# Three moves in one block kernel: attention queries asked for earlier, one stage put in program order, expert weights mixed one convolution earlier

## The chip, the cores and the metric

The kernel runs on one core of one Trainium2 chip. All data is float32. The metric is the device time of one execution in microseconds (us). The engines are named as in the profile: PE is TensorE (matrix products; PEld its weight loads), DVE is VectorE, ACT is ScalarE, POOL is GpSimd, SP is SyncE, which computes nothing and here only issues DMA transfers. Each engine takes its own instructions strictly in the order in which they were written into its stream. PSUM, which PE writes into, has 8 banks; a bank holds 512 float32 numbers in each of 128 partitions.

## What is computed

The input is three images of 256 channels on 48 x 48 pixels (2304 pixels each). Four layers follow, each of the form x = x + layer(norm(x)), where the norm is over 32 groups of channels:

```python
x = x + L0(gn(x))   # cv1 (1x1) + SiLU -> y1, y2; two blocks on y2; cv2 (1x1) on the concatenation + SiLU
x = x + L1(gn(x))   # 3x3 convolution whose kernel is a mix of 8 expert kernels, per image
x = x + L2(gn(x))   # plain 3x3 convolution
x = x + L3(gn(x))   # Mamba: scan over the 2304 pixels

# a block of L0:
cur = cur + attention(norm(cur))          # 4 heads of 32; the batch of 3 is used as q, k, v
cur = cur + f2 @ gelu(f1 @ norm(cur))     # MLP 128 -> 256 -> 128

# the mix of L1, for each image n:
routing = sigmoid(mean(x_n) @ routing_ws)             # 8 numbers
ws_n = sum over e of routing[e] * weight[e]           # 8 kernels of 256 x 256 x 3 x 3
```

A peculiarity of the attention: the leading axis of 3 of the projected tensor is split as if it were (q, k, v), so image 0 gives the queries, image 1 the keys and image 2 the values, and the three thirds of the channels (called g in the kernel) are the three attention problems.

## The kernel before

The layers run one after another. A chunk is 384 pixels of an image (6 chunks), in the attention up to 512.

**Attention (lines 520 to 660).** For each of two blocks there are 15 jobs: three groups g in the order 2, 1, 0, and for each five stretches of queries (four of 512, one of 256; `SCH`). A job goes through 18 groups of 128 keys (9 in the short jobs). In each group PE forms the scores of four heads (line 537), ACT takes the exponential (line 541), DVE adds the exponentials into `part` (line 608), and PE multiplies the exponentials with the values into the bank `acc` (line 550). The program writes "weighted" one group late (`behind`), so that PE has the next scores to do while ACT works. What a job leaves over is finished in the next job, at fixed groups: at group 0 DVE copies `acc` into `o` (line 590), at groups 1 and 3 PE sums the exponentials (`head_sums`, line 562), at group 4 ACT inverts the sums, at 5 DVE normalises, at 7 PE projects (line 506) and DVE adds to `cur` (line 508). The queries of the following job are formed at group 0: one product on PE (line 493) and one DVE instruction that takes it out of PSUM (`q`, line 498). All of `head_sums`, `queries`, `project` and the small norms share one PSUM bank, `ps_m`. In some jobs the statistics of the coming MLP (`mlp_weights`, called `aside`) are computed at groups 9, 11, 13 and so on.

The order of the attention is pinned: `keep_order` ties every instruction of PE, DVE, ACT and POOL to the one before it on the same engine, so each stream follows the program. Where nothing is pinned, a scheduler decides each engine's order.

**Last MLP and cv2 (lines 766 to 826).** For each image in the order 2, 1, 0: six chunks of 384 pixels of the MLP (`hidden`: two products and two Gelu on ACT; `add_back`: two products and one DVE add), then six chunks of cv2 (`concatenated`: eight products over four operands, two Silu on ACT, a POOL addition of the residual `xc`, two DVE statistics). Three of cv2's operands, `yc`, and the residual `xc` are fetched by `parts` two chunks ahead, by DMAs that SP issues. This stage is not pinned. After an image, `routing` computes its norm and its 8 mixing weights. The mixing (`mixed`) is a generator of 50 steps: 48 times, SP loads 384 KB of an expert kernel into one of six buffers (`wst`, line 238) and DVE multiplies and adds it into `u` (lines 262, 264); two last steps transform the kernel (lines 245 to 250). The kernel of image 2 is mixed while image 1 is in this stage, that of image 1 while image 0 is.

**Convolutions (lines 829 to 952).** Layers 1 and 2 use a Winograd transform along the rows. There are six units (layer 1 for images 2, 1, 0, then layer 2), each of two halves of 24 rows. For each half `input_transform` pads on POOL and ACT and makes six transformed inputs with 12 DVE instructions; `output` issues the products (line 888) and adds them into x with DVE. The generator `beside` runs other work next to a unit: next to unit 1 the mixing for image 0, next to unit 2 the loading of layer 2's kernel (`plain`).

**Mamba (from line 955).** It takes the second half of the time, is pinned, and is not touched by the change.

Of the kernel before, what the change touches and what calls it, by code (L numbers as in the profile page):

```python
# [9 lines left out]
F32 = mybir.dt.float32  # L10
# [6 lines left out]
P = 128  # L17
B = 3
HW = 48
# [10 lines left out]
TW = HW // 4  # L30
TAPS = 9
# [49 lines left out]
def net(  # L81
# [120 lines left out]
    def group_norm(b, psum, tag, stats=None):  # L202

        mv, gm, rstd = norm_stats([xs[b][:, ct, :] for ct in range(CT)], gmat, psum, tag, stats)
        sc = small.tile([P, CT], F32, name="gsc", bufs=4)
        nc.vector.tensor_copy(sc, rstd)
        sh = small.tile([P, CT], F32, name="gsh", bufs=4)
        nc.vector.scalar_tensor_tensor(sh, gm, -1.0, rstd, ALU.mult, ALU.mult)
        return mv, sc, sh

# [68 lines left out]

    def routing(b, psum, tag, stats):  # L280

        mv, sc, sh = group_norm(b, psum, tag, stats)
# [3 lines left out]
        nc.vector.tensor_tensor(pooled, pooled, sh, ALU.add)  # L286
        pr = psum.tile([P, 512], F32, tag=tag, name="ps_r")
# [10 lines left out]
    with ExitStack() as l0:  # L298
# [140 lines left out]
        with ExitStack() as p2:  # L439
# [9 lines left out]
            for i in range(NB):  # L449
# [40 lines left out]
                def queries(g, at, n):  # L490
# [6 lines left out]
                    q = work.tile([P, 512], F32, name="q")  # L497
# [14 lines left out]
                def attention(kts):  # L512
# [55 lines left out]
                    q = queries(jobs[0][0], *SCH[0])  # L568
                    old = behind = None
                    asides = {(1, 1): mlp_weights(i, 2), (0, 1): mlp_weights(i, 1)}  # L570
                    for at, job in enumerate(jobs):
# [6 lines left out]
                        for group in range(groups):  # L578
                            p = scores(job, kts[g], q, group)
# [11 lines left out]
                            if group == 0 and at + 1 < len(jobs):  # L591
                                q_next = queries(jobs[at + 1][0], *SCH[jobs[at + 1][1]])
# [10 lines left out]
                            if group == 9 and job == (1, 0):  # L603
                                kts[0] = keys(0)
                            if group >= 9 and group % 2:
                                next(aside, None)
# [10 lines left out]
                        q = q_next  # L617
# [151 lines left out]
        pss = l0.enter_context(tc.tile_pool(name="pss2", bufs=3, space=PSUM))  # L769
        psa = l0.enter_context(tc.tile_pool(name="psa2", bufs=1, space=PSUM))  # L770
        psm = l0.enter_context(tc.tile_pool(name="psm2", bufs=1, space=PSUM))
        wst = late_pool("wst", 6)

        def parts(b, c):

            yc = ypool.tile([P, 3, CH], F32, name="yc")
            nc.sync.dma_start(yc, ycat[b][:, :, c * CH : (c + 1) * CH])
            xc = ypool.tile([P, CT, CH], F32, name="xc")  # L780
            nc.sync.dma_start(
# [4 lines left out]
        def concatenated(b, c, yc, xc, stats):  # L786
# [13 lines left out]
            nc.gpsimd.tensor_tensor(both, both, xc, ALU.add)  # L800
            for m in range(2):
# [3 lines left out]
        mixing = iter(())  # L805
        upools = {}
        for n, b in enumerate(ORDER):
            xs[b] = late_pool(f"x{b}").tile([P, CT, N], F32, name=f"x{b}")
            ahead = []
            held = None  # L810
            for c in range(NCH):
# [4 lines left out]
                if n == 0 and c == 1:  # L816
                    at_once(mlp_weights(i, 0))
                if c >= NCH - 2:
                    ahead.append(parts(b, c - NCH + 2))
                for _ in range(4):  # L820
                    next(mixing, None)
# [4 lines left out]
            for c in range(NCH):  # L826
                if c + 2 < NCH:
                    ahead.append(parts(b, c + 2))
                concatenated(b, c, *ahead.pop(0), stats)
                for _ in range(5):  # L830
                    next(mixing, None)
            curpools[b].close()
            routing(b, psm, "m", stats)
            if n < 2:
                upools[n] = late_pool(f"up{n}")
                mixing = mixed(b, upools[n])


    with ExitStack() as l1:
        vp = l1.enter_context(tc.tile_pool(name="vp", bufs=2))  # L840
        pad = l1.enter_context(tc.tile_pool(name="pad", bufs=1))
# [3 lines left out]

        HR = HW // 2
        HN = HR * TW

        def input_transform(b, h, sc, sh):

            t = pad.tile([P, CT, HR + 2, PW], F32, name="xpad")
            zero = 0 if h == 0 else HR + 1
            nc.gpsimd.memset(t[:, :, zero, :], 0.0)
            for col in (0, PW - 1):
                nc.gpsimd.memset(t[:, :, :, col : col + 1], 0.0)
            lo = 1 if h == 0 else 0
            for ct in range(CT):
                src = xs[b][:, ct, :].rearrange("p (r c) -> p r c", c=HW)
                row = h * HR - 1 + lo
                nc.scalar.activation(  # L860
                    t[:, ct, lo : lo + HR + 1, 1 : PW - 1], src[:, row : row + HR + 1, :],
                    AF.Identity, bias=sh[:, ct : ct + 1], scale=sc[:, ct : ct + 1],
                )
            d = [t[:, :, :, k : k + 4 * TW - 3 : 4] for k in range(6)]
            vt = vp.tile([P, 6, CT, (HR + 2) * TW], F32, name="vt")
            o = [vt[:, i].rearrange("p t (r c) -> p t r c", c=TW) for i in range(6)]
            c = tmp.tile([P, CT, HR + 2, TW], F32, name="wc", bufs=1)
            e = tmp.tile([P, CT, HR + 2, TW], F32, name="we", bufs=1)
            tt, stt = nc.vector.tensor_tensor, nc.vector.scalar_tensor_tensor
            stt(c, d[2], -4.0, d[4], ALU.mult, ALU.add)  # L870
            stt(e, d[1], -4.0, d[3], ALU.mult, ALU.add)
            tt(o[1], c, e, ALU.add)
# [595 lines left out]
```

## Time and profile before

| | us |
|---|---|
| median of 5 runs | 3830.62 (3825.43 to 3839.13) |
| the profiled execution: its time | 3825.59 |
| the profiled execution: its span, first to last instruction | 3823.6 |
| first attention, first scores to last normalisation | about 113 to 737 |
| middle MLP and projections | about 737 to 810 |
| second attention | about 810 to 1430 |
| last MLP and cv2 | about 1430 to 1657 |
| convolutions | 1659 to about 2150 |
| Mamba | about 2150 to 3823 |

Over the whole span PE is busy for 3213.0 us (84%), DVE for 3226.7 (84%), ACT for 2228.3 (58%) and POOL for 1555.0 (41%). These shares are means over stages with different limits, so each stage is read by itself. Reading the lines: an instruction is named by its line, its engine and what it writes and reads (out<-in); "idle before, releaser" is how long its engine had nothing running just before it, and whose completion ended that. PEq, SPq and the like are an engine's sequencer, which issues DMAs and waits.

### The profile page before, as it was taken

The page shows a single profiled execution, that of the slowest core. Times are in us where ns is not written, and L with a number is a line of the kernel's source. Part 1 is how long each engine was busy: PE and PEld are TensorE (multiplying, and loading weights), DVE is VectorE, ACT ScalarE, POOL GpSimd, SP SyncE. Part 2 cuts the span into 40 slices and gives each one's busy share as a digit, 9 for nine tenths or more (in the row PEclk, how much of TensorE's full clock was granted, in tenths as well). Part 3 has the DMA queues.
Part 4 walks back from the last instruction along what each step waited for, and adds up shares of the span by engine and source line. Part 5 has one row for each costly group of instructions (what it writes and reads, how often), then busy time and mean ns, then how long its engine had stood idle before and what let it go on. Part 6 is the DMA issues. An engine that isn't in the chain of part 4 may idle for free. (4 is left out here: it accounts for less than half of the span.)

```text
span 3823.6 us, 45652 instructions
## 1 busy us (share of the span) xinstructions
PE 3213.0 (84%) x17010; PEld 1402.8 (37%) x17010; DVE 3226.7 (84%) x3518; ACT 2228.3 (58%) x3216; POOL 1555.0 (41%) x674
## 2 busy tenths in 40 slices
PE   7999999999999998678799757877778878887874
PEld 4323232432323234356577523333333333333331
DVE  4798889768888985799988349999998999999997
ACT  2787777657877773210000147676677666777663
POOL 0000000000000001100000049999999999999998
PEclk9999999999999999889899878888888888888886
DMA  4000000000000006824100133434343433343441
GB/s 183 3 1 2 1 1 1 22 36 1 2 1 1 1 1 197 302 76 161 38 32 35 59 80 93 111 92 109 100 104 92 108 92 100 101 111 98 105 101 34
DMA packets 149962, 266.50 MB, mean 70 GB/s; under 512 B 23441, under 2 KB 123601, under 8 KB 147170
## 3 DMA queue, kind: packets, MB, share of 16 engines
q1 hardware_dynamic: 149730, 263.49, 24.2%
q8 instruction: 135, 2.21, 0.2%
q14 instruction: 97, 0.79, 0.1%
HBM read 216.31 MB, written 46.89 MB: 69 GB/s over the span
## 5 line engine op out<-in xcount | busy, mean ns | idle before, releaser
L541 ACT ACTIVATE pt<-ps_s 128x1024 f32<-128x1024 f32 x972 | 939.2, 1022 | 257.7 <-PE ps_s L537 239.6
L1336 POOL TENSOR_TENSOR hc<-hs,bc 128x1536 f32<-128x1536 f32 x288 | 991.1, 3442 | 82.1 <-DVE hs L1321 52.8
L608 DVE TENSOR_TENSOR part<-part,pt 128x2048 f32<-128x2048 f32 x396 | 906.8, 2290 | 104.5 <-ACT pt L541 77.1
L1321 DVE TENSOR_TENSOR_SCAN hs<-ps_da,hst,hs 128x384 f32<-128x384 f32 x960 | 909.5, 997 | 24.3 <-ACT ps_da L1265 20.9
L1265 ACT ACTIVATE ps_da<-dtr,amat 128x384 f32<-128x384 f32 x1152 | 657.3, 581 | 359.9 <-DVE hs L1321 343.3
L158 POOL TENSOR_TENSOR rstd<-ve,mhalf 128x2 f32<-128x2 f32 (+1 forms) x26 | 17.7, 682 | 1680.3 <-DVE ve L156 1680.3
L537 PE MATMUL ps_s<-q,kt 32*128 32x512 f32 (+1 forms) x4320 | 613.9, 593 | 1.8 <-DVE q L498 0.9
L1253 POOL TENSOR_TENSOR hs<-dtur,bc 128x768 f32<-128x768 f32 x288 | 523.8, 1819 | 77.1 <-DMA dtr<-dtd 77.1
L550 PE MATMUL acc<-pt,vt 128*32 128x512 f32 (+1 forms) x4320 | 522.2, 562 | 3.3 <-DVE o L590 3.1
L888 PE MATMUL ps_c<-vt,u 128*128 128x288 f32 x1728 | 430.1, 412 | 35.7 <-DVE u L250 31.8
L1066 PE MATMUL ps_g<-xn,wtap 128*128 128x384 f32 x1152 | 393.1, 494 | 36.4 <-ACT u L1073 31.2
L888 PEld LDWEIGHTS ps_c<-vt,u 128*128 128x128 f32 x1728 | 331.8, 193 | 128.7 <-DVE u L250 32.8
L537 PEld LDWEIGHTS ps_s<-q,kt 32*128 32x128 f32 x4320 | 219.6, 183 | 389.0 <-issue 234.9
L1281 PE MATMUL ps_y<-hc,rep 128*32 128x384 f32 x2304 | 294.9, 598 | 37.1 <-POOL hc L1336 35.2
L1252 DVE TENSOR_TENSOR hs<-ps_r,bc 128x768 f32<-128x768 f32 x288 | 268.7, 933 | 60.5 <-PE ps_r L1234 60.5
L1066 PEld LDWEIGHTS ps_g<-xn,wtap 128*128 128x128 f32 x1152 | 213.2, 190 | 220.8 <-ACT u L1073 54.9
L550 PEld LDWEIGHTS acc<-pt,vt 128*32 128x32 f32 x4320 | 97.5, 108 | 354.6 <-issue 339.4
L904 ACT COPY cb<-ps_c 128x288 f32<-128x288 f32 x48 | 19.0, 395 | 334.6 <-PE ps_c L888 324.9
L1321 DVE TENSOR_TENSOR_SCAN hs<-ps_da,hs 128x384 f32<-128x384 f32 x192 | 170.5, 935 | 16.1 <-ACT ps_da L1265 16.1
L1137 PE MATMUL ps_g<-xn,w3sb 128*128 128x384 f32 x288 | 130.9, 596 | 57.5 <-ACT sz L1145 43.2
L1030 PE MATMUL ps_g<-xg,mean 128*128 128x384 f32 x72 | 52.7, 887 | 105.2 <-ACT dt L1128 78.2
L1281 PEld LDWEIGHTS ps_y<-hc,rep 128*32 128x32 f32 x2304 | 51.5, 118 | 241.1 <-POOL hc L1336 112.3
(204 smaller groups left out, 3263.1 us busy)
## 6 DMA issues: line engine op xcount, KB each, us to landing
wconv<-in_we SPq DMA_DIRECT2D x144, 384.0 KB, 4.6
dtr<-dtd SPq DMA_DIRECT2D x288, 192.0 KB, 3.6
bc<-bcd SPq DMA_DIRECT2D x144, 192.0 KB, 5.8
dtur<-dtud SPq DMA_DIRECT2D x288, 96.0 KB, 2.7
dtd<-dt SPq DMA_DIRECT2D x18, 768.0 KB, 3.5
yc<-ycat SPq DMA_DIRECT2D x18, 576.0 KB, 5.3
xb<-in_x SPq DMA_DIRECT2D x6, 1152.0 KB, 11.2
xc<-in_x SPq DMA_DIRECT2D x18, 384.0 KB, 7.1
```

Of the source, the lines that this page charges most:

```text
L537: nc.tensor.matmul(s[:, j, cols], kt[r, mt * P : (mt + 1) * P], q[r, :n], start=True, stop=True,)
L541: nc.scalar.activation(p[:, h0 : h0 + 2, :], s, AF.Exp)
L550: nc.tensor.matmul(acc[h * HD : (h + 1) * HD, :n], vt[:, mt, g * P + h * HD : g * P + (h + 1) * HD], p[:, h, cols], start=mt == 0, stop=mt ...
L608: nc.vector.tensor_tensor(part, first_p if group == 1 else part, p, ALU.add)
L888: nc.tensor.matmul(pc[:, :HN], u[:, i, dy, ct, m * P : (m + 1) * P], vt[:, i, ct, dy * TW : dy * TW + HN], start=ct == 0 and dy == 0, stop ...
L1066: nc.tensor.matmul(bank[:, m % 2, :CH], wtap[:, tap, ct, m * P : (m + 1) * P], k.xn[:, ct, tap : tap + CH], start=tap == 0 and ct == 0, st ...
L1252: nc.vector.tensor_tensor(hs[:, 0:2, :], k.ps[:, :, :CH], bb, ALU.mult)
L1253: nc.gpsimd.tensor_tensor(hs[:, 2:4, :], k.rows[m][1], bb, ALU.mult)
L1265: nc.scalar.activation(da[:, :CH], chunks[at].rows[m][0][:, q, :], AF.Exp, scale=amat[:, col : col + 1])
L1281: nc.tensor.matmul(k.y_ps[32 * q : 32 * q + 32, :CH], fold, hc[:, q, :], start=False, stop=g == 3,)
L1321: nc.vector.tensor_tensor_scan(hs[:, q, :], decays[q][:, :CH], hs[:, q, :], 0.0 if k.c == 0 else state[m, g][:, q : q + 1], ALU.mult, ALU.add,
L1336: nc.gpsimd.tensor_tensor(hc, hs, cb, ALU.mult)
```

## The change

1. The queries of a job are formed at group 10 of the job before it, no longer at group 0. A short job has only 9 groups; so the fourth long job of a third, which precedes it, also forms those of the job after the short one, at group 13. A third buffer holds them. The asides move from groups 9, 11, 13, ... to 11, 13, ..., and `keys(0)` from group 9 to 11.
2. The last MLP and cv2 stage is pinned with `keep_order`. `parts` is issued by ACT instead of SP, three chunks ahead over the images' borders, and first of all for three chunks at the stage's start. The PSUM banks are dealt out anew (two pairs instead of three for the products; three banks instead of one for `acc`). The statistics of a chunk are written behind the next chunk's products. `routing` and `mlp_weights` become generators, of which each chunk runs one step (`aside`).
3. In that stage only the kernel of image 2 is mixed, at 2 steps per chunk of the MLP and 3 per chunk of cv2, from the moment that its routing is known. The kernel of image 1 is mixed beside unit 0 (image 2), and that of image 0 beside unit 1, as before. The first input transform (image 2, first half) is moved into the stage, to the fourth cv2 chunk of image 0.

The diff, cut to its core (`input_transform` itself is moved in the file and unchanged but for the pool of its two scratch tiles):

```diff
+            yield          # in routing, after `pooled`; its norm is a generator too
...
-                    q = work.tile([P, 512], F32, name="q")
+                    q = work.tile([P, 512], F32, name="q", bufs=3)
...
-                    q = queries(jobs[0][0], *SCH[0])
+                    asked = {}
+                    def ask(at):
+                        if at < len(jobs):
+                            g, c = jobs[at]
+                            asked[at] = queries(g, *SCH[c])
+                    ask(0)
...
-                            p = scores(job, kts[g], q, group)
+                            p = scores(job, kts[g], asked[at], group)
...
-                            if group == 0 and at + 1 < len(jobs):
-                                q_next = queries(jobs[at + 1][0], *SCH[jobs[at + 1][1]])
...
-                            if group == 9 and job == (1, 0):
+                            if group == 10:
+                                ask(at + 1)
+                            if group == 13 and c == len(SCH) - 2:
+                                ask(at + 2)
+                            if group == 11 and job == (1, 0):
                                 kts[0] = keys(0)
-                            if group >= 9 and group % 2:
+                            if group >= 11 and group % 2:
                                 next(aside, None)
...
-        pss = l0.enter_context(tc.tile_pool(name="pss2", bufs=3, space=PSUM))
-        psa = l0.enter_context(tc.tile_pool(name="psa2", bufs=1, space=PSUM))
+        pss = l0.enter_context(tc.tile_pool(name="pss2", bufs=2, space=PSUM))
+        psa = l0.enter_context(tc.tile_pool(name="psa2", bufs=3, space=PSUM))
...
-            nc.sync.dma_start(yc, ycat[b][:, :, c * CH : (c + 1) * CH])
+            nc.scalar.dma_start(yc, ycat[b][:, :, c * CH : (c + 1) * CH])
             xc = ypool.tile([P, CT, CH], F32, name="xc")
-            nc.sync.dma_start(
+            nc.scalar.dma_start(
                 xc, x[b, :, c * CH : (c + 1) * CH].rearrange("(t p) n -> p t n", p=P)
             )
...
+        mark = listed[-1]
+        chunks = [(b, c) for b in ORDER for c in range(NCH)]
+        ahead = [parts(*chunks[z]) for z in range(3)]
+        small_steps = [mlp_weights(i, 0)]
+        mixing = mixed(2, upools[0])
+        def aside(n):
+            if small_steps:
+                try:
+                    next(small_steps[0])
+                except StopIteration:
+                    del small_steps[0]
+            if 2 in route:
+                for _ in range(n):
+                    next(mixing, None)
         for n, b in enumerate(ORDER):
             held = None
             for c in range(NCH):
                 f = hidden(b, c)
                 if held is not None:
                     add_back(i, *held)
                 held = b, c, f
-                if n == 0 and c == 1:
-                    at_once(mlp_weights(i, 0))
-                if c >= NCH - 2:
-                    ahead.append(parts(b, c - NCH + 2))
-                for _ in range(4):
-                    next(mixing, None)
+                aside(2)
             add_back(i, *held)
...
             for c in range(NCH):
-                if c + 2 < NCH:
-                    ahead.append(parts(b, c + 2))
-                concatenated(b, c, *ahead.pop(0), stats)
-                for _ in range(5):
-                    next(mixing, None)
-            curpools[b].close()
-            routing(b, psm, "m", stats)
-            if n < 2:
-                upools[n] = late_pool(f"up{n}")
-                mixing = mixed(b, upools[n])
+                concatenated(b, c, *ahead.pop(0))
+                z = n * NCH + c + 3
+                if z < len(chunks):
+                    ahead.append(parts(*chunks[z]))
+                if c:
+                    take_stats(b, c - 1, stats)
+                if b == 0 and c == 3:
+                    vp = late_pool("vp", 2)
+                    pad = late_pool("pad")
+                    first_v = input_transform(2, 0, *norms[2])
+                aside(3)
+            take_stats(b, NCH - 1, stats)
+            if b:
+                curpools[b].close()
+            small_steps.append(routing(b, psm, "m", stats))
+        for _ in mixing:
+            pass
+        keep_order(tc, listed, mark)
+        for steps in small_steps:
+            at_once(steps)
...
-        beside = {1: mixed(ORDER[2], upools[0]), 2: plain(upools[1])}
+        beside = {0: mixed(1, upools[1]), 1: mixed(0, upools[0]), 2: plain(upools[1])}
...
-        vt = transformed(0)
+        vt = first_v
```

## The prediction

> **What bounds the kernel now.** I read the busy shares by slices first, then the waits of each stage, then the order of instructions at the places that the change touches, and last the busy time of DVE over the stretch that the mixing spans. The Mamba stage (from 2150 us) keeps its instructions and their order; nothing is summed there.
>
> The attention: its waits (first attention; us in total, times, longest), then two borders between jobs in order of time (start, us, engine, what, idle before).
>
> ```profile
> PE ps_m L562 <- DVE q L498: 17.3, 10, 2.1
> ...
> 202.77 0.68 DVE L590 COPY o<-acc 128x512 f32<-128x512 f32 x1
> 203.37 0.74 DVE L498 TENSOR_SCALAR q<-ps_m,qkb 128x512 f32<-128x512 f32 x1
> 204.16 1.06 PE L562 MATMUL ps_m<-pt,ones 128*32 128x512 f32 x8 [1.64 <-DVE q L498]
> 204.53 2.29 DVE L608 TENSOR_TENSOR part<-pt 128x2048 f32<-128x2048 f32 x1 [0.42 <-ACT pt L541]
> ...
> 710.81 0.68 DVE L590 COPY o<-acc 128x512 f32<-128x512 f32 x1
> ...
> 711.54 1.09 PE L550 MATMUL acc<-pt,vt 128*32 128x256 f32 x16 [1.57 <-DVE o L590]
> ```
>
> PE hardly ever waits inside a job; at each border it waits some 1.7 us, because `head_sums` needs the bank that DVE has not yet emptied of the queries. The last border (711 us) has no queries, and there PE waits 1.57 us all the same: for `o`, which DVE copies only when its additions are done. So DVE's lag is behind the wait, and the queries only stand in front of it.
>
> The cv2 stage and the first convolutions: waits of the stage, then waits of the convolutions, then busy time from the first mixing instruction to unit 2's first product.
>
> ```profile
> PE ps_s L790 <- DMA yc<-ycat: 30.1, 6, 14.3
> ...
> SPq L238 <- DVE u L264: 65.3, 71, 3.3
> ...
> PE ps_c L888 <- DVE u L250: 31.8, 1, 31.8
> ...
> core 0: us, PE busy (x) PEld busy (x) DVE busy (x) ACT busy (x) POOL busy (x), PEclk, DMA share, GB/s
> 1492.40:1835.85 343.45, 241.29 (x854) 165.22 (x854) 316.62 (x425) 56.28 (x79) 29.90 (x32) 0.87 0.54 188
> 1656.00:1835.85 179.85, 142.96 (x582) 111.08 (x582) 173.98 (x250) 19.46 (x27) 3.62 (x16) 0.91 0.29 101
> 1880.00:2146.00 266.00, 252.83 (x1028) 196.56 (x1028) 211.92 (x384) 28.48 (x43) 6.83 (x20) 0.97 0.07 25
> ```
>
> PE's waits here are for operands behind SP's queue and for mixed kernels; but DVE is busy for 316.6 of 343.5 us, and PE for only 241. From 1492 to 1836 us this is a DVE stretch with 26.9 us of slack. From 1880 us PE is the bound (252.8 of 266), and starts when this stretch lets it.
>
> **Part 1, the queries.** Per border the product (1.06) and the DVE instruction (0.745) go from group 0 to group 10. They are not removed, so their own time is worth nothing; what may go is the wait, about 1.73 at 20 borders (17.3 in each attention), with 1.57 for `o` at the two last ones. What is late next? Take a long job and call the start of its first scores T (198.25 in the trace; the next job starts at 243.16, so a period is 44.9). Before, the third scores start at T + 7.77 (206.02). Without product and wait they start at T + 5.02 (two scores of 1.07, two weighted products of 1.0, `head_sums` 0.88). All until the fourth addition follows them: it starts at T + 16.14 now (214.39), so at T + 13.39. From there DVE runs without a pause for 33.3 us up to `o` (247.68), and now has 0.745 for the queries on top: `o` is finished at 13.39 + 34.04 + 0.68 = T + 48.1. PE needs it 4.02 after its next start, and that is at T + 44.9 - 1.64 = T + 43.3, so at T + 47.3. A wait of 0.8 remains in place of 1.64; delaying a job by it delays both sides alike, so it repeats. Gain 0.83 per border, 12 borders in each attention (those out of a short job have none): 24 x 0.83 = 20. Bounds: the whole wait goes, 20 x 1.73 + 2 x 1.57 = 38; or `o` takes it as at 711 us, 24 x (1.73 - 1.57) = 4. I take **-20**, since the lag is counted from this trace's own rows. The asides at groups 11 to 17 keep their four steps; `keys(0)` has until the last third.
>
> **Part 2, pinning, ACT's loads, banks.** Before the stage six loads stand in front of ACT's first Gelu. A yc takes 5.3 us to land (median), and by the order of instructions the fourth load waits for the first one's semaphore, the sixth likewise. The first Gelu therefore ends at about 1441 us, not 1433.5; the two pairs of banks are full by then, and PE loses about 5 us (before, it is dense here). At every step from cv2 to the next image the xc load waits on ACT for POOL's addition:
>
> ```profile
> 1474.79 1.23 ACT L795 ACTIVATE x<-ps_s,cv2sh,cv2sc 128x384 f32<-128x384 f32 x2 [3.93 <-PE ps_s L790]
> 1476.10 1.81 POOL L800 TENSOR_TENSOR x<-x,xc 128x768 f32<-128x768 f32 x1 [3.35 <-ACT x L795]
> 1477.94 0.38 SPq L781 DMA_DIRECT2D xc<-in_x  x1
> ...
> 1479.95 1.23 ACT L795 ACTIVATE x<-ps_s,cv2sh,cv2sc 128x384 f32<-128x384 f32 x2 [3.93 <-PE ps_s L790]
> ```
>
> Inside cv2 that is hidden: Silu 1.23, addition 1.81, issue 0.38 and some 0.3 of signalling are 3.7 of a chunk's 5.16 us on PE. At the image's end nothing hides it: the table load (1.28) and the first Gelu pair (1.05) stand behind it, so the first `add_back` can start 6.2 after the last cv2 product, with PE having 2.6 of other products: 3.6 us lost twice. In exchange the waits on yc (30.1) should go: a yc has 10.3 - 1.5 = 8.8 us from its issue to its use, 10.0 being the longest landing before.
>
> Routing now runs one step per chunk. After image 2's last product the first `add_back` ends at 7.5 us, two more chunks with their steps at 13.3, the DVE add and the two broadcasts before the routing products at 14.6, these at 15.3, the Sigmoid at 15.9. Before it was 12.6 (1479.75 to 1492.36). Image 2 ends at about 1484 (5 us lost, small products in line), so DVE's first mixing instruction moves from 1492.4 to **1500**.
>
> **Part 3, the mixing.** It removes no DVE instruction: one mixing (48 x about 1.04 plus 12 x 0.96, some 60 us) goes from the stage to the side of unit 0, and an input transform (12 instructions, 13.2 us) from the convolutions into the stage. PE's path to the point where DVE starts that transform, from image 2's end at 1484: MLP of image 1 21.8 (the 15.3 above and five products of 1.29 left), cv2 6 x 5.16 = 31, MLP of image 0 24 (the same and two mixing steps in front of each routing step), four cv2 chunks 20.6, Silu and two paddings (1.39 each) 4.2: 1585.6. DVE has by then 45 mixing steps (48), nine additions of 0.61, eighteen statistics of 0.55 and routing, 67.5 us in 85.6: **18 idle**. The rest of its ledger follows without pause, as in the trace where it is full for 174.0 of 179.9 us. The ledger: 316.6, less 4.6 because 48 steps leave POOL's neighbourhood (1.15 each in the stage, 1.04 beside the convolution). So 312 - 67.5 = 244.5, and 3 idle while unit 0 fills its banks: unit 2 starts at 1585.6 + 247.5 = 1833, against 1835.85. PE waits for u(2) at about 1590 to 1611, then twice for the next kernel where it waited once; none of it counts, since DVE sets the pace. Sum **-3**. Bounds: no later start and 10 us less idle give -22; the 30.1 of waits on yc staying, on top of the -3, give +27.
>
> The Trainium skill, "DMA: Bandwidth & Descriptors", section "Issuing engines are not separate DMA queues", speaks against the ACT loads: all issuing engines end on the same 16 DMA engines, so a second issuer saves only issue time. The row it is held against: SP sat 65.3 us waiting for DVE before expert loads, with yc behind them in its order. By the rule alone the 30.1 would stay and part 3 would read +27; by the row it goes, and part 3 reads -3. I go by the row.
>
> **Sum.** -20 - 3 = -23 against the profiled execution's 3825.6 (span 3823.6): 3802.6. That execution lies 5 below the median of the five runs; against the median it is 3807.6, so **3808**.
>
> **The rivals.**
> - *Both in full*: the wait goes altogether (-38) and the stage has little DVE idle (-18): about 3774. For it: PE is dense in the stage before, and 401 GB/s have been reached, so loads need not bind. Against: DVE's additions fill the job, and the ledger leaves at most 27.
> - *Nothing moves*: `o` takes the whole wait (-4), the stage gives 0: 3827. For it: the border at 711 us. Against: that border follows a job whose own start was delayed by queries.
> - *Slower, through one mechanism*: the pinned DVE. A late expert load stops not only the mixing but the statistics, `add_back` and routing steps written behind it, and PE with them; before, the scheduler had put other work there. Price: every us by which the transform at 1585.6 is late goes straight into the end. With the DMA share at 0.9 or more as from 1580 to 1630 us (330 GB/s), and 3 x 393 KB + 983 KB per cv2 chunk of 5.16 us asking for 419 GB/s, each of nine such chunks would take 6.5 us: 12 in all; the loads' collisions of before cost 30.1. It decides from 23 on, where it has eaten the -20 and the -3; at 31 it gives 3838.
> - The change does what it says: the streams' order shows it, so "no effect by construction" has no chance.
>
> **How the numbers follow.** My case (3795 to 3822) 0.55; both in full 0.13; nothing moves 0.14; slower 0.18. 0.2% of the time, 7.7 us, is about what a measurement of this kernel can tell from no change. Faster by more: 0.55 + 0.13 = 0.68, less 0.02 for the top of my range; same: 0.14 and a little of both neighbours, 0.16; slower: 0.18. Range: 3784 leaves out the deeper half of "both in full", 3836 the worse half of "slower".
>
> **What the profile after should show.** Waits of `ps_m` on q gone; in their place `acc` on `o` at 0.8 us per border, jobs of 44.1 us. First Gelu of the stage near 1441 less the attention's gain, and 3 to 4 us of PE idle at each change of image. No long wait on yc. First convolution product about 1611 less that gain; two waits of PE on `u` L250 of 30 us or more, and unit 2's start about 23 us earlier. I am wrong if PE still waits over 1.3 us at the borders, if DVE is idle for over 35 us between mixing and unit 2, or if ACT's loads hold Gelu up by 10 us.

## The result, and the profile after

| | before | after |
|---|---|---|
| median, us | 3830.96 (47 runs) | 3836.51 (26 runs, 3828.08 to 3842.33) |
| ratio after to before, 95% interval | | 1.0014 (1.0009 to 1.0019) |
| profiled execution: its time | 3825.59 | 3847.11 |
| profiled execution: its span | 3823.6 | 3845.4 |

The changed kernel is 5 us slower; 3808 was forecast. By the bound named in the forecast (7.7 us) this is no change; the interval shows that it is not faster. The profiled execution of after lies 10.6 above its median and above the highest of its 26 runs, that of before 5.4 below its median, so the two traces differ by 21.8 where the medians differ by 5.5: sizes from the traces say where time went, sizes of whole edits come from the ratios. In the traces the 21.8 are made of -20.3 up to the last scores of the attention, +37.5 from there to the first product of unit 2, +1.9 to the last convolution product and +2.7 behind it. So the attention did what was forecast, and a larger loss sat in the stage that I had put down as -3.

Attention: the scores' group of before and of after (range of starts in us), then PE's waits in the first attention of after, and one border.

```profile
L537 PE MATMUL ps_s<-q,kt x4320: 374/587/1056, 114.4 to 1425.6; 32*128 32x512 f32 x158, 32*128 32x256 f32 x39
```

```profile
L583 PE MATMUL ps_s<-q,kt x4320: 374/587/1218, 115.2 to 1405.3; 32*128 32x512 f32 x158, 32*128 32x256 f32 x39
...
PE acc L596 <- DVE o L643: 4.0, 7, 1.3
...
203.42 1.07 PE L596 MATMUL acc<-pt,vt 128*32 128x512 f32 x8 [0.44 <-DVE o L643]
```

The waits for `q` (17.3 in the first attention before) are gone. What took their place is the wait for `o`: 4.0 at seven borders, 0.44 at the one shown.

The stage: PE's waits in it (us in total, times, longest), the chunks of one MLP in order of time (start, duration), and a change of image.

```profile
PE ps_s L469 <- ACT f L473: 24.2, 17, 5.9
PE ps_c L927 <- DVE u L257: 21.8, 1, 21.8
PE ps_m L818 <- DVE ext L816: 6.5, 1, 6.5
...
1430.58 1.45 PE L479 MATMUL acc<-f,w0b 128*128 128x384 f32 x4
1430.78 0.58 ACT L473 ACTIVATE f<-ps_s,fb 128x384 f32<-128x384 f32 x1 [1.00 <-PE ps_s L469]
1431.87 0.28 PE L189 MATMUL ps_gv<-gd,mean 128*128 128x1 f32 x2
1432.01 0.89 PE L469 MATMUL ps_s<-cur,wf 128*128 128x384 f32 x2
1433.00 0.58 ACT L473 ACTIVATE f<-ps_s,fb 128x384 f32<-128x384 f32 x1 [1.64 <-PE ps_s L469]
1433.63 0.91 PE L469 MATMUL ps_s<-cur,wf 128*128 128x384 f32 x2 [0.73 <-ACT f L473]
1434.38 1.45 PE L479 MATMUL acc<-f,w0b 128*128 128x384 f32 x4
...
1478.87 0.38 ACTq L839 DMA_DIRECT2D xc<-in_x  x1
1479.28 1.28 ACT L473 ACT_TABLE_LOAD   x1 [2.31 <-POOL x L858]
1480.57 0.58 ACT L473 ACTIVATE f<-ps_s,fb 128x384 f32<-128x384 f32 x1
...
1481.20 2.93 PE L469 MATMUL ps_s<-cur,wf 128*128 128x384 f32 x4 [4.87 <-ACT f L473]
```

PE's row at 1433.63 carries the case. It is the second product of a chunk, and it waits for the Gelu of the first product of the *same* chunk: `hidden` writes product, Gelu, product, Gelu, and both products go into the two halves of one tile `ps_s`. PE can't go on to anything else, because the stage is pinned. From one `add_back` to the next it is 3.80 us (1430.58 to 1434.38) with a small product of the statistics between, and 3.58 without one (1438.41 to 1441.99), where I had counted four passes of 0.645, 2.58.

There is a second loss, which the waits do not show: the granted clock. Busy times (columns as in the block below; PEclk, the last column but two, is 1.00 at full speed) of the MLPs of images 1 and 0 in after, of two stretches inside the first of them, then of image 0's MLP in e2 (below), and of the stage's first 48 us in before:

```profile
1475.53:1510.91 35.38, 24.67 (x57) 12.30 (x56) 10.41 (x27) 13.52 (x19) 2.51 (x2) 0.76 0.25 78
1541.87:1578.94 37.07, 25.11 (x58) 12.31 (x57) 20.11 (x37) 13.52 (x19) 2.80 (x2) 0.77 0.61 213
1481.20:1485.00 3.80, 3.06 (x5) 1.31 (x5) 0.00 (x0) 1.16 (x2) 0.00 (x0) 0.50 0.08 29
1501.00:1506.00 5.00, 4.64 (x7) 2.52 (x8) 0.39 (x1) 0.89 (x2) 0.00 (x0) 0.50 0.46 152
...
1520.88:1543.46 22.58, 17.18 (x57) 9.76 (x56) 20.01 (x37) 12.70 (x19) 2.80 (x2) 1.00 0.89 312
...
1430.74:1479.00 48.26, 47.99 (x156) 28.03 (x155) 14.51 (x38) 16.40 (x26) 9.60 (x6) 1.00 0.47 144
```

The products of one MLP keep PE busy for 17.2 us at a granted clock of 1.00, and for 24.7 and 25.1 at 0.76 and 0.77. Behind PE's longer waits in this stage (6.5 for `ext`, a small check at the stage's start, then 4.9, 2.0, 5.9 and 2.0) the clock is 0.50; behind the short ones of 0.73 it stays at 0.99 (1428.00 to 1445.00).

From DVE's first mixing instruction to unit 2's first product, whole and in its two parts (busy us and instructions of each engine), and the waits of the convolutions:

```profile
core 0: us, PE busy (x) PEld busy (x) DVE busy (x) ACT busy (x) POOL busy (x), PEclk, DMA share, GB/s
1498.86:1603.69 104.83, 90.12 (x249) 49.71 (x248) 62.61 (x88) 32.09 (x45) 21.79 (x14) 0.89 0.72 246
1603.69:1853.05 249.36, 155.46 (x605) 116.90 (x603) 246.12 (x327) 23.24 (x32) 8.01 (x18) 0.81 0.45 155
1498.86:1853.05 354.19, 245.59 (x853) 166.61 (x851) 308.74 (x414) 55.32 (x77) 29.79 (x32) 0.83 0.53 182
...
1631.82 12.10 PE L927 MATMUL ps_c<-vt,u 128*128 128x288 f32 x38 [21.75 <-DVE u L257]
...
1744.46 35.82 PE L927 MATMUL ps_c<-vt,u 128*128 128x288 f32 x137 [32.41 <-issue]
...
1853.05 7.31 PE L927 MATMUL ps_c<-vt,u 128*128 128x288 f32 x18 [34.22 <-DVE u L257]
```

From the first transform on (1603.69) DVE is full, 246.1 of 249.4 us, as forecast (247.5). All that was lost lies ahead of it: in 104.8 us DVE is busy for 62.6. DVE does not set the pace there; PE does, in single file with ACT, and DVE reached that transform 38.4 us late.

### The profile page after: what moved, and what is told of

Read it like the earlier page. It is cut to its first block, busy times and chain, and to the rows that moved or that the text cites. A ratio compares the mean times of both kernels' runs of the same rounds, so it can differ in the third digit from the quotient of the medians.

```text
span 3845.4 us, 45642 instructions
## 1 busy us (share of the span) xinstructions
PE 3231.3 (84%) x17010; PEld 1408.0 (37%) x17010; DVE 3221.1 (84%) x3518; ACT 2227.5 (58%) x3216; POOL 1554.9 (40%) x674
## 5 line engine op out<-in xcount | busy, mean ns | idle before, releaser
L1360 DVE TENSOR_TENSOR_SCAN hs<-ps_da,hst,hs 128x384 f32<-128x384 f32 x960 | 909.7, 997 | 24.3 <-ACT ps_da L1304 19.9
```

The lines of the kernel that those rows point to most:

```text
L1360: nc.vector.tensor_tensor_scan(hs[:, q, :], decays[q][:, :CH], hs[:, q, :], 0.0 if k.c == 0 else state[m, g][:, q : q + 1], ALU.mult, ALU.add,
```

## The experiments

Three explanations of the lost 37 us stood against each other. A: the pinned order makes the chunk's second product wait. B: ACT's loads hold up its Gelus. C: DVE's pinned order (my fourth case). Two more questions were whether the attention's gain is real outside one execution, and what the loads and the mixing are worth by themselves. Ratios are to the kernel before on the same chip, with 95% intervals; the last four columns are worked out from each run's trace: from the last scores to the first mixing instruction, from the last scores to unit 2's first product, and the stretch between those two with DVE's idle time in it.

| run | median us | ratio | mixing | unit 2 | stretch | DVE idle |
|---|---|---|---|---|---|---|
| before | 3830.96 | | 66.8 | 410.3 | 343.5 | 26.8 |
| after | 3836.51 | 1.0014 (1.0009 to 1.0019) | 93.6 | 447.8 | 354.2 | 45.4 |
| e1: part 1 alone | 3804.04 | 0.9930 (0.9918 to 0.9943) | 66.8 | 412.5 | 345.7 | 27.5 |
| e2: products ahead of Gelus | 3805.47 | 0.9941 (0.9928 to 0.9953) | 79.7 | 412.7 | 333.0 | 24.3 |
| e3: no pin | 3787.10 | 0.9891 (0.9877 to 0.9906) | 68.8 | 389.8 | 321.0 | 9.7 |
| e4: SP's loads | 3823.13 | 0.9984 (0.9975 to 0.9994) | 78.1 | 427.1 | 349.0 | 39.3 |
| e5: e2 and SP's loads | 3803.29 | 0.9931 (0.9917 to 0.9944) | 70.2 | 409.7 | 339.5 | 30.8 |
| e6: no pin, SP's loads | 3790.04 | 0.9895 (0.9880 to 0.9910) | 68.6 | 393.0 | 324.4 | 14.9 |
| e7: no pin, part 3 undone | 3790.38 | 0.9897 (0.9882 to 0.9912) | 68.8 | 394.1 | 325.3 | 9.7 |
| e8: no pin, products ahead | 3789.54 | 0.9891 (0.9876 to 0.9906) | 69.4 | 393.3 | 323.9 | 13.1 |
| e9: e1, loads further ahead | 3796.92 | 0.9913 (0.9901 to 0.9926) | 66.7 | 404.4 | 337.7 | 23.9 |
| e10: e2, DVE free | 3810.73 | 0.9948 (0.9934 to 0.9962) | 76.0 | 411.2 | 335.2 | 28.9 |
| e11: after, DVE free | 3832.50 | 1.0006 (0.9998 to 1.0015) | 92.4 | 441.4 | 349.0 | 42.3 |
| e12: e5 with DVE filled | 3794.80 | 0.9895 (0.9879 to 0.9912) | 70.3 | 401.4 | 331.1 | 18.3 |

**e1, part 1 alone.** The kernel before with the change's edits in the attention and nothing else:

```diff
-                            if group == 0 and at + 1 < len(jobs):
-                                q_next = queries(jobs[at + 1][0], *SCH[jobs[at + 1][1]])
...
+                            if group == 10:
+                                ask(at + 1)
+                            if group == 13 and c == len(SCH) - 2:
+                                ask(at + 2)
```

> The kernel before with part 1 alone (the queries at group 10, asked one job ahead). Theory A (the attention gained what the trace says, the loss is all in the last stage): both attentions 10 us shorter each, the rest as before, about 3811 us, 0.995 of before. Rival (the attention's gain is not real outside the profiled execution, since the whole kernel came out only 5 us slower and not 20): 3825 to 3830. Rival (the stage loses because it starts earlier, whatever its order): attention 20 shorter and the first mixing instruction more than 67 us behind the last scores.

Measured: 0.9930, 27 us faster (22 to 31); its profiled execution has a span of 3803.6, 20.0 shorter than before's. The attention's gain is real, and by itself it is the forecast's -20 or a little more. The stage that follows is not disturbed by starting earlier: mixing at 66.8 behind the last scores, as before. So parts 2 and 3 together cost what lies between e1 and after: 0.9930 to 1.0014, some 32 us.

**e2, both products ahead of both Gelus**, in the last stage of the changed kernel:

```diff
             for m in range(2):
                 nc.tensor.matmul(
                     pf[:, m, :CH], wf[:, m * P : (m + 1) * P], chunk(cur[b], c),
                     start=True, stop=True,
                 )
-                nc.scalar.activation(f[:, m, :], pf[:, m, :CH], AF.Gelu, bias=fb[:, m : m + 1])
+            for m in range(2):
+                nc.scalar.activation(f[:, m, :], pf[:, m, :CH], AF.Gelu, bias=fb[:, m : m + 1])
```

> The changed kernel; in the last stage the two products of an MLP chunk are written ahead of its two Gelus instead of product, Gelu, product, Gelu. Theory A (the pinned order makes the chunk's second product wait for the first one's Gelu, because both halves lie in one tile; a chunk then takes 4.0 us of PE's time instead of 2.58): chunks of 2.6 to 2.8 us, 18 chunks at 1.3 us less, so unit 2 starts 20 to 25 us earlier and the whole is 3811 to 3817 us. Theory B (ACT's loads hold the Gelus): chunk and time stay as in the changed kernel, 3836. Theory C (DVE with its fixed order sets the pace of the stage): PE's waits move to DVE, the time stays within 5 us of 3836.

Measured: 0.9941, some 28 us less than after by the ratios. PE's waits in its stage, and its MLP chunks in order of time:

```profile
PE ps_m L822 <- DVE ext L820: 6.6, 1, 6.6
PE acc L483 <- ACT f L477: 5.7, 2, 3.0
...
1428.59 1.54 PE L469 MATMUL ps_s<-cur,wf 128*128 128x384 f32 x4
1429.96 1.45 PE L483 MATMUL acc<-f,w0b 128*128 128x384 f32 x4
1431.25 1.45 PE L469 MATMUL ps_s<-cur,wf 128*128 128x384 f32 x4
1432.54 2.74 PE L483 MATMUL acc<-f,w0b 128*128 128x384 f32 x8
```

The 24.2 us of waits for `f` (17 times) are 5.7 (twice), and from `add_back` to `add_back` it is 2.58 us (1429.96 to 1432.54), the value that the forecast had used. Nothing but the place of one ACT instruction per chunk was changed. A holds, and more goes than its 3811 to 3817 had: the long waits shrink with the short ones. The forecast's ledger holds to some 5 us: first transform 164.1 us behind the last scores (forecast 160.0, after 198.4), unit 2 at 412.7 (forecast 407.4, after 447.8), median 3805.5 (forecast 3808).

**e3, no pin in the stage**; banks, ACT's loads and mixing as changed:

```diff
         for _ in mixing:
             pass
-        keep_order(tc, listed, mark)
```

> The changed kernel without the fixed order in the last stage; banks, ACT's loads and the mixing stay as changed. Theory A (pin): the scheduler puts other products into the wait between a chunk's two products, as it did before; the first mixing instruction comes 70 us behind the last scores instead of 93.5, unit 2 starts some 20 us earlier: about 3815 us. Theory B (ACT's loads): still 3830 to 3840. Theory C (DVE's fixed order): as A by the time, but then the MLP chunks stay at 4 us of PE and the DVE idle time shrinks.

Measured: 0.9891, the fastest of all, some 47 us under after by the ratios and 42 under before: better than my A had it. Busy times from the first mixing to unit 2 (columns as above):

```profile
1474.70:1795.71 321.01, 235.35 (x848) 162.64 (x846) 311.27 (x414) 55.00 (x77) 31.09 (x32) 0.88 0.58 201
```

DVE does the same work as in the pinned kernel (311 against 309 us, 414 instructions in both) in 321 us instead of 354. So the pin costs more than the chunk waits, and without it the other edits are a gain over e1 of 15 us by the ratios, 17 by the medians. e5 to e12 ask after these two remainders.

**e4, SP's loads** in the changed kernel:

```diff
-            nc.scalar.dma_start(yc, ycat[b][:, :, c * CH : (c + 1) * CH])
+            nc.sync.dma_start(yc, ycat[b][:, :, c * CH : (c + 1) * CH])
...
-            nc.scalar.dma_start(
+            nc.sync.dma_start(
                 xc, x[b, :, c * CH : (c + 1) * CH].rearrange("(t p) n -> p t n", p=P)
             )
```

> The changed kernel with the parts yc and xc issued by SP again; the rest as changed. Theory A: MLP chunks stay at 4.0 us; what goes is the first Gelu's delay (6 us) and 3 to 4 us at each change of image, 12 at most, against waits for yc behind the expert loads in SP's order, up to 30: 3825 to 3850 us. Theory B (ACT's loads are the main loss): about 3805 us, with chunks of 2.6 us.

Measured: 0.9984, 3823.1 us, 11 us under after by the ratios and 2 us under A's range. B falls as the main cause: PE still waits for `f`. (In the traces unit 2 is 20.7 us earlier; after's trace is the one that lies high.) Its wait in the stage, and ACT's first table load there in order of time:

```profile
PE ps_s L469 <- ACT f L473: 18.6, 17, 2.6
...
1409.33 1.28 ACT L473 ACT_TABLE_LOAD   x1
```

What went is what the forecast had priced: the first Gelu's table load starts 6.1 us behind the last scores instead of 12.5 (1409.33 and 1417.79 in their traces), and the longest wait at a change of image is 2.6 instead of 5.9. And no wait for yc appears, although SP issues these loads again.

**e5, e2 with SP's loads.** The two edits of e2 and e4 together.

> Pinned, the two products of a chunk written ahead of its Gelus, and yc and xc issued by SP. Theory A (chunk waits were worth 31 us, ACT's loads some 10 of their own): e2's 3805.5 less the first Gelu's delay (6 us) and what is left at the image changes (2.7 and 3.0 us): 3794 to 3800 us. Rival (the 13 us that SP's loads gained in e4 were the same time as the chunk waits): 3803 to 3808 us. Rival (with the stage faster, yc comes late behind the expert loads in SP's order): over 3810.

Measured: 0.9931, 2 to 4 us under e2 with intervals that overlap, at the edge of the first rival. The first mixing instruction comes 9.5 us earlier (70.2 against 79.7), but unit 2 only 3.0: the rest turned into DVE idle time (30.8 against 24.3). Loads on ACT and chunk waits overlap in their effect; with the chunks dense, the issuer is worth next to nothing.

**e6, no pin and SP's loads.** The edits of e3 and e4 together; against e3 it differs by the issuing engine alone.

> No fixed order in the last stage, and yc and xc issued by SP; mixing and banks as changed. This is the disputed queue alone. Theory A (the row of before: PE waits 30 us for yc behind SP's expert loads): the waits on yc come back and the time is 20 to 30 us above e3's 3787, so 3807 to 3817. Rival (three chunks ahead is enough, whoever issues; the rule that all issuers end on the same DMA engines): 3780 to 3790 us, without long waits on yc.

Measured: 0.9895, 3 us over e3 and within its interval; PE has no wait for yc at all, its longest wait for ACT in the stage is 1.0. My reason for part 2, that ACT's queue rids PE of the 30 us, falls here: with the second mixing out of the stage, they are gone with SP as well.

**e7, no pin, part 3 undone:** both mixings in the stage and the transform behind it, ACT's loads and banks as changed.

```diff
-        mixing = mixed(2, upools[0])
+        def mixes():
+            yield from mixed(2, upools[0])
+            while 1 not in route:
+                yield
+            yield from mixed(1, upools[1])
+        mixing = mixes()
...
-        beside = {0: mixed(1, upools[1]), 1: mixed(0, upools[0]), 2: plain(upools[1])}
+        beside = {1: mixed(0, upools[0]), 2: plain(upools[1])}
...
-        vt = first_v
+        vt = transformed(0)
```

> No fixed order, ACT's loads and banks as changed, but the second mixing inside the stage and the first input transform behind it, as in the kernel before: part 3 undone. Theory A (DVE's work from the first mixing to unit 2 is the same whichever way, so the mixing's place is worth some 3 us, and the 17 us by which e3 beats e1 come from the loads): 3785 to 3793 us. Rival (the mixing's place is what gained): 3800 to 3806, as e1.

Measured: 0.9897, 3 us over e3, within its interval. The mixing's place by itself is worth nothing that can be seen, as the ledger had it (-3). PE's wait for yc:

```profile
PE ps_s L848 <- DMA yc<-ycat: 2.7, 1, 2.7
```

**e8, no pin and products ahead of Gelus.** The edits of e2 and e3 together.

> No fixed order, and the two products of a chunk ahead of its Gelus. Theory A (the scheduler already fills the wait between the two products): within 4 us of e3's 3787. Rival (the wait costs without the pin too): 3770 to 3780 us.

Measured: 0.9891, the same as e3 to the fourth digit. Where a scheduler may put other products between the two, the wait costs nothing; it is pin and emission order together that cost.

**e9, e1 with the loads further ahead**, issued by SP, the rest as before:

```diff
+        chunks = [(b, c) for b in ORDER for c in range(NCH)]
+        ahead = [parts(*chunks[z]) for z in range(3)]
...
-                if c >= NCH - 2:
-                    ahead.append(parts(b, c - NCH + 2))
...
-                if c + 2 < NCH:
-                    ahead.append(parts(b, c + 2))
                 concatenated(b, c, *ahead.pop(0), stats)
+                z = n * NCH + c + 3
+                if z < len(chunks):
+                    ahead.append(parts(*chunks[z]))
```

> The kernel before with part 1, and yc and xc issued by SP, three chunks ahead of their use in one row over all three images (before: up to two ahead, beginning anew with every image). No pin, banks, statistics, routing and mixing as before. Theory A (the 17 us by which the unpinned versions beat e1 are the waits for yc behind the expert loads, which go when the parts are asked for earlier, whoever asks): 3784 to 3792 us, waits on yc under 8 us instead of 30. Rival (they come from the other banks, the later statistics or the routing in steps): 3800 to 3806, as e1.

Measured: 0.9913, 6 us under e1, between the two expectations and with intervals that overlap. The waits for yc have not gone:

```profile
PE ps_s L798 <- DMA yc<-ycat: 30.1, 4, 23.0
```

So asking earlier is not what removes them when SP issues and both mixings are in the stage; the scheduler still leaves the yc behind expert loads in SP's order (25 of them from 1553.27 to 1582.24, the yc at 1582.29). With e6 and e7 this gives three readings with no pin: both mixings in the stage and SP's loads 30.1 us of waits; both in the stage and ACT's loads 2.7; one in the stage and SP's loads none. It looks as if either edit were enough; but e9 also has before's banks, statistics and routing, so this comparison is not a clean one, as that of e3 with e6 is. From e9 to e7, with all these differences, 27 us of PE's waits go and the time falls by 6 us.

**e10 and e11, DVE free.** e2, and the changed kernel, with PE, ACT and POOL pinned in the stage and DVE left to the scheduler:

```diff
-def keep_order(tc, listed, mark):
+def keep_order(tc, listed, mark, dve=True):
...
+        if e == mybir.EngineType.DVE and not dve:
+            continue
```

> e2 (both products of a chunk ahead of its Gelus) with PE, ACT and POOL pinned in the last stage and DVE left to the scheduler. Theory A (what the pin costs beyond the chunk waits, 16 to 18 us, is DVE idle in its fixed order, with statistics and add-backs ahead of mixing steps that could run): 3788 to 3793 us, DVE idle from the first mixing to unit 2 some 12 us instead of 24. Rival (it is PE's or ACT's fixed order, the first mixing instruction 80 us behind the last scores instead of 69): 3800 to 3806.

> The changed kernel with DVE alone left to the scheduler; PE, ACT and POOL pinned as changed. Theory A (the chunk's second product waits for its first Gelu, and this is between PE and ACT, whatever DVE's order): chunks stay at 4 us of PE, 3818 to 3830 us. Rival (DVE's fixed order was the main loss, as my fourth case had it): 3785 to 3800 us.

Measured: 0.9948 (3810.7 us, above both expectations) and 1.0006 (3832.5, a little above A's). Freeing DVE gains 3 us in the changed kernel, with intervals that overlap, and nothing with dense chunks. C falls as I had it: the pin on DVE is not what holds the stage up. In e11 the chunks are as slow as before it (PE waits 27.6 us for `f`, 17 times). DVE's order itself is not cleared by this, for the order that the scheduler gave it was no better. DVE's longest waits from the first mixing to unit 2, in e2, e10 and e3:

```profile
DVE xst L866 <- POOL x L862: 14.5, 6, 3.8
...
DVE xst L866 <- POOL x L862: 19.9, 7, 4.2
...
DVE u L271 <- DMA wconv<-in_we: 4.3, 8, 1.3
DVE xst L862 <- POOL x L858: 3.4, 2, 1.7
```

In e10 DVE still stands before statistics whose operand POOL has not finished, and more than in e2.

**e12, e5 with more work for DVE beside the stage:**

```diff
-                aside(2)
+                aside(3)
...
-                if b == 0 and c == 3:
+                if b == 0 and c == 0:
...
-                aside(3)
+                aside(4)
```

> e5 (pinned, both products of a chunk ahead of its Gelus, SP's loads) with one mixing step more per chunk (3 and 4 instead of 2 and 3) and the first input transform at image 0's first cv2 chunk instead of its fourth. What the pin still costs is 13 to 16 us against the unpinned versions. Theory A (in its order DVE has too little written beside the stage: from 1475 to 1566 us it was busy for 63.1 of 91 us in e5, and for 84.3 in e3 without the pin): 3785 to 3793 us, DVE idle from the first mixing to unit 2 at 10 to 15 us instead of 31. Rival (PE's and ACT's order sets the stage's end, DVE only waits for it): 3800 to 3806. Rival (more steps per chunk ask for more expert weights than the DMA engines bring, and the pinned add-backs wait behind the mixing): over 3806.

Measured: 0.9895 against e5's 0.9931; 3794.8 us and 18.3 us of DVE idle time, both just outside A's ranges. Busy times over the same stretch of time (columns as above), first in e5, then in e12, then in e3:

```profile
1475.00:1566.00 91.00, 83.57 (x250) 48.27 (x249) 63.06 (x88) 31.09 (x45) 21.88 (x14) 0.94 0.84 284
```

```profile
1475.00:1566.00 91.00, 74.08 (x218) 42.62 (x217) 77.09 (x95) 28.60 (x42) 18.15 (x12) 0.89 0.77 270
```

```profile
1475.00:1566.00 91.00, 78.13 (x231) 43.56 (x230) 83.96 (x106) 32.89 (x45) 20.56 (x16) 0.94 0.81 291
```

DVE is busy for 77.1 of these 91 us instead of 63.1, and unit 2 starts 8.3 earlier; the ratios say 14 us, with intervals that lie apart, the medians 8.5 (before is 4 us slower on e12's chip). So a good part of what the pin still cost was that the order, as it was written, gave DVE too few mixing steps per chunk: the steps written beside a chunk are all that DVE has until the next one. The expected start of the transform did not come (1566.6 against 1565.6 in e5: the added mixing steps took its place), so the steps did it, not the transform. In its trace e12 is still 11.6 behind e3 at unit 2. One wait of PE for DVE's statistics, 12.9 us at 1530, is longer than any in e5 (4.6), but e3 has one of 12.0 too. By the ratios hardly anything is left (0.9895 and 0.9891). This rest was not taken further.

The versions without the pin beat both kernels; e3, the changed kernel less one line, is the fastest at 3787.1 us, with e6, e7, e8 and e12 inside its interval.

## Why the prediction was wrong

*Part 1 was right in reason, and in its sum partly by luck.* Forecast -20; the last scores come 20.3 earlier, and e1 by itself is 20.0 shorter in its trace (27 by the ratio). The wait that follows was named rightly, `o` in place of `q`, but over-sized: 0.8 at twelve borders of each attention forecast, 9.6 in all; in the first attention 4.0 at seven borders, six of 0.25 to 0.71 and one of 1.3. So its waits fell by 14.9 (17.3 and 1.6 to 4.0) and its time by 10.6; what took the other 4 was not looked into. From one copy into `o` to the next the gain is 0 to 1.5, not 0.83 or nothing.

*The step that failed is "MLP of image 1 21.8 (the 15.3 above and five products of 1.29 left)", and with it "MLP of image 0 24" and the 1484 for image 2's end.* All three use a chunk of 2.58 us on PE, a duration from a trace in which the scheduler had interleaved other products. Under the pin it is 3.58, or 3.80 with a small product in it. In the trace of after, image 1's MLP takes 35.4 from the last cv2 product (1475.53 to 1510.91) and image 0's 37.1 (1541.87 to 1578.94), and image 2 ends 11.8 later than forecast, less the attention's gain: 13.6 + 13.1 + 11.8 = 38.5 of the 38.4 by which the transform is late. Its core is the chunk: product 0.65, wait for its end and its Gelu, 1.62 in all from 1432.01 to 1433.63, before the second product may start. Worked out from after's rows, as an estimate: 1.00 too much per chunk makes 18 for 18 chunks. The table loads add some 5: 4.9 and 5.9 us of PE idle at the two changes of image where 3.6 was forecast, and 2.0 at each Sigmoid of the routing, which the pin puts between two Gelus. The clock behind the longer waits, a term that the forecast did not have at all, adds some 17: PE was busy for 33.3 us at 0.50 to 0.52, and at 1.00 half of that would have done. Together that is about 40, with the 5 in it that the forecast had at the stage's start. The three hang together: e2, which only lets PE go on inside a chunk, takes away 34.3 of the 38.4. How much the clock is worth alone no run shows, nor why it falls: in e2 one wait of PE, 2.7 us, is followed by 0.54 (1471.80 to 1478.50) and the other, 3.0 us, by 1.00. The profile of before could have told the first part:

```profile
1430.74 2.20 PE L423 MATMUL ps_s<-cur,wf 128*128 128x384 f32 x6
...
1433.00 1.05 ACT L427 ACTIVATE f<-ps_s,fb 128x384 f32<-128x384 f32 x2
```

PE's first row of the stage is three products (two instructions each), all ahead of the first Gelu. As a chunk's second product waits for its first Gelu, they can only be the first products of three chunks.

*The remainder of part 3 was right.* From the transform to unit 2 249.4, forecast 247.5; no long wait for yc; first Gelu ended at 1419.7, forecast 1441 - 20.3; two waits of over 30 us ahead of units 1 and 2, though the profile puts only the second down to `u`. e2, with the chunk as I had taken it, gives 3805.5 for a forecast of 3808. That it comes so near is partly luck: by the ratios part 1 is worth 27 and not 20, and e2 lies 4 us above e1 (intervals overlap) where part 3 had -3. Two terms of the sum are off by their own numbers and move little: 48 steps at 1.15 against 1.04 are 5.3 and not 4.6, and the bound of -22 adds up to some -20.6 (3, 7.6 and 10).

*The slower rival had the right side and the wrong mechanism.* Late loads stopping a pinned DVE: in after, DVE waits 2.4 us for expert weights, and e11 shows that its pin is worth 3 us. The mechanism was PE's pin, together with the order in which `hidden` writes.

*The rule and the row.* The Trainium skill, "DMA: Bandwidth & Descriptors", section "Issuing engines are not separate DMA queues", says that a second issuing engine saves only the time of issuing. I had gone by the row, SP's queue, against it. The runs give each its case: with the second mixing out of the stage the issuer makes no difference that can be seen (e3 and e6), as the rule has it; with both mixings in the stage 30.1 us of waits with SP stand against 2.7 with ACT (e9 and e7, which differ in more than the issuer), where the rule alone would leave them. What neither said is the cost on ACT's side, which the forecast had added of its own: 11 us in the pinned kernel (e4).

*Open:* what gives the 15 us by which the unpinned versions beat e1, since neither the issuer (e6) nor the mixing's place (e7) nor, by more than 6 us, the earlier loads (e9) is worth them alone (the other banks, the later statistics and the routing in steps were not tried singly). The traces say where they went: from the first mixing to unit 2, DVE in e1 waits 8.1 us for POOL's x before statistics and 7.7 for PE's `acc`, in e3 3.4 and 0.6, in e7 not at all. That points to the later statistics and the three banks of `acc`; it is not shown. Open too is why the traces of before and after differ by 16 us more than their medians.

## What to carry to other kernels

Pinning turns the emission order of a helper into the schedule: before pinning a stage, read each helper as one engine's single file, and put the instructions that free a tile behind all products that go into it. A duration per chunk taken from an unpinned trace includes what the scheduler put between; for a pinned stage, add up the dependent chain instead (product, its end, Gelu, second product), and read the granted clock of each stretch beside its waits, as in after the products behind waits of 2 to 6.5 us took twice their time. And whoever pins must also hand-fill: what is not written beside a chunk, the idle engine will not find.

## What was not expected of the hardware

A DMA that a computing engine issues costs it more than the issue. The first three loads of yc and xc on ACT stand ahead of the first Gelu, and one waits for an earlier load to land. ACT's rows of the changed kernel in order of time:

```profile
1417.14 0.62 ACTq L839 DMA_DIRECT2D xc<-in_x  x1
1417.79 1.28 ACT L473 ACT_TABLE_LOAD   x1 [6.38 <-DMA yc<-ycat]
```

Counted from the last scores, the first table load of the changed kernel starts 6.4 us later than with SP's loads (12.5 against 6.1 in e4). A delay of some 7 us was forecast; that removing it from a dense stage (again 6.4 us between e2 and e5) moves the end by only 2 to 4 us was not: the time reappeared as DVE's idle time.
